# A graph layer on one core: the last group of edges gets an order of its own

## The chip, the cores and the metric

The kernel runs on one NeuronCore of a Trainium2 chip. The core has five engines with instruction queues of their own: TensorE (PE in the profile, its weight loads as PEld), VectorE (DVE), ScalarE (ACT), GpSimd (POOL) and SyncE (SP). SP, ACT and POOL also issue DMAs, which 16 DMA engines carry out. The metric is the device time of one execution in microseconds (us), lower is better; of several runs the median is taken.

## What is computed

A message-passing layer on a graph with 6250 nodes of 128 features and 206250 edges, sorted by receiver, and a residual with a layer norm behind it:

```
w_ij  = silu(edge_feats @ rad_W1 + rad_b1) @ rad_W2 + rad_b2
w_ij += silu(chi_scalar @ sph_W1 + sph_b1) @ sph_W2 + sph_b2
q_i = (x @ Wq)[receivers];  k_j = (x @ Wk)[senders];  v_j = (x @ Wv)[senders]
alpha = (q_i * w_ij * k_j).sum(over the 16 of a head) / sqrt(16) * cutoffs
out = segment_sum(alpha * v_j, receivers) / 16
result = layernorm(x + out)
```

There are 8 heads of 16. `edge_feats` and `chi_scalar` are the two arrays of 206250 x 32 edge attributes, `cutoffs` the edge weights. Everything is float32.

## The kernel before

**Tiles.** 128 edges are a tile, 4 tiles a quad (512 edges), 4 quads a group (2048 edges). The 206250 edges make 403 quads and 101 groups (`NG`); the last group, 100, has three quads: 400, 401 and 402. A group's quads are worked in the order 0, 2, 1, 3 (`order`), so the last three are 400, 402, 401. As the edges are sorted by receiver, the receivers of a quad lie within a window of 32 nodes (`W`), and those of a group within one of 128, and the windows of neighbouring groups overlap.

**First stage.** A table `kv_tab` with the keys and values of all nodes is made and stored in HBM; those of the first ten quads are made from gathered rows of x instead.

**Main loop** (from line 603, over groups and the four slots of each). All instructions are issued in an order written out by hand; each engine runs its own in that order and waits by semaphore for the others. In the iteration of quad `order[i]`:
- TensorE works the first layers of quad i+2 (`first_layers`, L408), fetches the queries of quad i+1 to its edges with a one-hot product (`q_at_edges`, L419) and works the second layers of quad i+1 (`weigh`, L450 and L455).
- ACT takes the SiLU of quad i+2 (`silus`, L440).
- DVE multiplies query and key of quad i+1 (`multiply`, L462, reads the gathered `kv`), and then of quad i multiplies by the weights, sums over the heads, scales (`scores`, L469 to L473) and makes the messages (`messages`, L484).
- POOL gathers the 4 x 128 rows of `kv_tab` for quad i+14 (`gathers`, L120, `AHEAD`), each row gather after a signal of TensorE from quad i.
- In slots 1 to 3 TensorE sums the messages of the group before into the windows of its quads (`sum_quads`, L495, one-hots of 32 columns from `one_hots`); ACT copies the sums (`part_sums`, L524).

**From sums to rows.** `place(g)` makes two matrices on DVE (L518, L519) that move a group's four windows, and the total of the group before it, into the group's window of 128 rows. `sum_group(g)` multiplies with them on TensorE (L529, L531), and ACT copies the total `tot` (L533). `statistics(g)` adds x and takes mean and variance on DVE (L541 to L544). Four groups are a batch (`LB`): after the fourth, ACT takes the square roots (L547), DVE reciprocal and shift (L549, L551), and ACT scales the rows (L554). The batches are groups 0 to 3, 4 to 7 and so on up to 92 to 95; then 96 and 97 together, then 98, 99 and 100 each alone. The square root and SiLU need different function tables on ACT, so each batch brings a table load before its square root and another before the next SiLU. `write_rows` lets SP write a group's 128 rows to `out` (L561), one group a slot. Since the windows overlap, each write waits for the one before it to land.

**The last group** is handled by conditions on `last` in the same loop. Its quads aren't summed into windows of 32: `wide_one_hots(q)` (L503, L504, L507) makes one-hots of 128 columns, kept in buffers of the tag `act`, and `sum_wide` (L511) sums straight into the 128 rows of the group. The wide one-hots are made at the end of slot 3 of group 99 (quad 400), in slot 0 (402) and in slot 1 (401) of the last group; `place(99)` in slot 0, `place(100)` (one matrix) in slot 1. There also stands the load of a verdict into a register of each engine (line 658): whether the inputs are of the assumed form; if not, a slower general path follows. In the last group's slot 2 quad 402 is finished, with the statistics of group 98. Behind the loop (line 672 on) come the sums of group 99, the last quad's scores and messages in two halves (its multiply was done whole before), the statistics of group 99 between the halves, and the statistics and the write of group 100 (L708, L710).

Of the kernel before, what the change touches and what calls it, by code (L numbers as in the profile page):

```python
# [24 lines left out]
P = 128  # L25
# [29 lines left out]
def gnn_kernel(ctx, tc, x, src, dst, weight, edges, rad_W1, rad_b1, rad_W2, rad_b2,  # L55
# [310 lines left out]
    with tc.tile_pool(name="ps", bufs=1, space=PSUM) as pp:  # L366
# [93 lines left out]
        def multiply(q, mark=None):  # L460
            kq_of[q] = quad_of("kq", 3)
            o = nc.vector.tensor_tensor(kq_of[q], pq_of[q], kv_of[q][:, :, :D], op=OP.mult)  # L462
            if mark is not None:
                after(o, mark)
# [34 lines left out]
        def wide_one_hots(q):  # L499
# [5 lines left out]
            hot_of[q, "wide"] = ep.tile([P, EQ], F32, name="act", bufs=8).rearrange(  # L505
# [8 lines left out]
        def place(g):  # L514

            to = to_of[g] = gp.tile([P, 2, P], F32, name="to")
# [18 lines left out]
        def statistics(g):  # L535
            first = g // LB * LB if g < NG - 3 else g
            if g == first:
                y0_of[g] = (gp.tile([P, LB, D], F32, name="y0"), gp.tile([P, LB, 2], F32, name="mv"))
            y0, mv = y0_of[first]
            k = g - first + 1  # L540
            nc.vector.tensor_tensor(y0[:, k - 1, :], tot_of[g], x_of[g], op=OP.add)  # L541
            st = gp.tile([P, 6], F32, name="st")
            nc.vector.bn_stats(st, y0[:, k - 1, :])
            nc.vector.bn_aggr(mv[:, k - 1, :], st)  # L544
            if k == LB or g >= NG - 4:
                sd = gp.tile([P, LB], F32, name="sd")
                nc.scalar.activation(sd[:, :k], mv[:, :k, 1], AF.Sqrt, bias=eps)  # L547
                rs = gp.tile([P, LB], F32, name="rs")
                nc.vector.reciprocal(rs[:, :k], sd[:, :k])  # L549
                shift = gp.tile([P, LB], F32, name="shift")  # L550
                nc.vector.scalar_tensor_tensor(shift[:, :k], mv[:, :k, 0], -1.0, rs[:, :k],  # L551
                                               op0=OP.mult, op1=OP.mult)
                for i in range(k):
                    nc.scalar.activation(y0[:, i, :], y0[:, i, :], AF.Identity,  # L554
                                         scale=rs[:, i:i + 1], bias=shift[:, i:i + 1])
                    written.append((first + i, y0[:, i, :]))
# [46 lines left out]
        for g in range(NG):  # L603
            last = g == NG - 1
            for slot, j in enumerate((0, 2, 1, 3)):
                q = g * NQ + j
                i = g * NQ + slot
                if q >= QUADS:
                    continue
# [3 lines left out]
                if slot == 0 and g + 1 < NG:  # L613
# [3 lines left out]
                if slot == 2 and g + 1 < NG:  # L617
                    turned = make_q(g + 1)
                if 1 <= g:
                    for t in ((), (0, 1), (2, 3))[slot] if last else ((), (0, 1), (2,), (3,))[slot]:  # L620
                        mark = sum_quads(g - 1, t)
                if last and slot == 2:
                    po_of[g] = pp.tile([P, EQ], F32, name="ph", bufs=2)[:, :D]
                    for t in range(QT):
                        sum_wide(order[i - 2], t, start=(t == 0))
                if i + 2 < len(order):
                    first_layers(order[i + 2])
                if i + 1 < len(order):
                    mark = q_at_edges(order[i + 1])
                    marks = weigh(order[i + 1])  # L630
                if i + 2 < len(order):
                    silus(order[i + 2], mark, marks)
# [6 lines left out]
                if i + 1 < len(order):  # L639
                    multiply(order[i + 1], mark)  # L640
                    messages(q, scores(q, marks=marks), marks=marks)
# [6 lines left out]
                if slot == 1:  # L648
                    if g + 1 < NG:
                        one_hots_T(g + 1)  # L650
                    if g + 2 < NG:
                        pick(g + 2)
                    if 1 <= g < NG - 1:
# [215 lines left out]
```

## Time and profile before

| | us |
|---|---|
| median of 3 runs | 2042.45 (2042.1 to 2043.92) |
| the run that was profiled | 2043.99 |
| its span, from the first to the last instruction | 2042.2 |
| busy: PE | 1843.1 (90%) |
| busy: PEld | 1527.2 (75%) |
| busy: DVE | 1466.9 (72%) |
| busy: ACT | 720.1 (35%) |
| busy: POOL | 1529.6 (75%) |
| DMA engines, mean share | 50% (queue of gathers 36.1%, of SP's transfers 13.8%) |

A page of the profile has the busy time of each engine, the groups of instructions, the chain of work that ended last, and the waits. A line of the groups reads: source line, engine, operation, the tile written and those read, shapes, count, then busy us and the mean ns of one, and after the last bar the idle time of the engine just before them with what ended most of it. A line of the timeline reads: start in us from the span's beginning, duration, engine, source line, operation, tiles, shapes, count, and in square brackets the idle time before it and what ended it. A line of the waits reads: who waited for what, us in total, how many times, the longest. On the span's last stretches the table by windows gives these busy times and granted TensorE clocks:

| us from the start | PE | DVE | ACT | POOL | granted clock |
|---|---|---|---|---|---|
| 1980 to 2000 | 18.06 | 13.62 | 9.93 | 15.12 | 0.83 |
| 2000 to 2020 | 17.37 | 14.23 | 6.19 | 15.12 | 1.00 |
| 2020 to 2042.2 | 11.06 | 14.94 | 6.92 | 2.53 | 0.80 |

### The profile page before, as it was taken

Reading aid. Unit: us, or ns where it says so; the run is one execution under the profiler, and the core shown is the slowest. Engines: PE = TensorE matmul, PEld = TensorE weight load, DVE = VectorE, ACT = ScalarE, POOL = GpSimd, SP = SyncE. Lnnn points to the kernel's source line nnn. Section 1 sums busy time; section 2 is a strip of 40 time slices with the busy share of each in tenths; the row PEclk is TensorE's granted clock in tenths of the full one; section 3 lists DMA queues with packets and bytes.
Section 4 is the critical chain, followed back from the end, with each engine's and each line's share of the span. In section 5 each row is a group of like instructions: output and inputs, shape, how many; then the busy total and the mean of one; then the engine's idle time right before and its main releaser. Section 6 shows DMA issues by size and latency. Waiting matters only on the chain.

```text
span 2042.2 us, 44162 instructions
## 1 busy us (share of the span) xinstructions
PE 1843.1 (90%) x16011; PEld 1527.2 (75%) x16011; DVE 1466.9 (72%) x3005; ACT 720.1 (35%) x1425; POOL 1529.6 (75%) x1620
## 2 busy tenths in 40 slices
PE   9999998889899999898999989898998999898987
PEld 7788887777777777777777777777776777777776
DVE  6698887677767677677767667776766767677766
ACT  2334443333333323333333333233333333333333
POOL 7777777777777777777777777777777777777774
PEclk9899999899898898899888988998989989989889
DMA  8555554545445544545454554445454544544452
GB/s 309 149 150 154 154 157 145 153 136 152 140 147 141 153 146 142 146 143 152 136 151 142 149 148 145 146 142 148 140 152 136 153 140 148 151 143 147 140 149 81
DMA packets 141371, 304.03 MB, mean 149 GB/s; under 512 B 34028, under 2 KB 73820, under 8 KB 141148
## 3 DMA queue, kind: packets, MB, share of 16 engines
q0 software_dynamic: 76736, 208.77, 36.1%
q1 hardware_dynamic: 62912, 92.00, 13.8%
q8 instruction: 127, 2.08, 0.4%
q14 instruction: 96, 0.79, 0.1%
q10 hardware_dynamic: 1500, 0.40, 0.1%
HBM read 287.58 MB, written 13.46 MB: 147 GB/s over the span
## 4 chain that ended last, share of the span: by engine, by line
PE 50%; DMA 19%; DVE 14%; issue 7%; ACT 4%; POOL 4%; DVEq 0%; POOLq 0%; ACTq 0%
PE pw L455 24%; DMA kv<-kv_tab,src_i 19%; PE pq L419 10%; PE ph L408 7%; DVE kq L462 5%; PE po L495 4%; DVE side L471 2%; DVE kq L469 2%; PE pw L450 2%; POOL kv L120 2%; POOL msg L120 2%; ACT y L554 2%; ACT L440 2%; PE pq L388 1%; PE pq L529 1%
## 5 line engine op out<-in xcount | busy, mean ns | idle before, releaser
L120 POOL DMA_INDIRECT kv<-kv_tab,src_i x1572 | 1489.9, 948 | 479.7 <-issue 188.9
L440 ACT ACTIVATE act<-ph,b 128x512 f32<-128x512 f32 x806 | 518.7, 685 | 1176.6 <-PE pq L419 1149.0
L455 PE MATMUL pw<-w,act 128*128 128x128 f32 x6448 | 911.1, 300 | 0.1
L455 PEld LDWEIGHTS pw<-w,act 128*128 128x128 f32 x6448 | 830.1, 208 | 105.5 <-issue 93.2
L462 DVE TENSOR_TENSOR kq<-pq,kv 128x512 f32<-128x512 f32 x403 | 277.6, 689 | 401.6 <-DMA kv<-kv_tab,src_i 225.1
L419 PE MATMUL pq<-q,hotT 32*128 32x128 f32 x3224 | 498.1, 297 | 29.6 <-DVE kq L462 28.8
L408 PE MATMUL ph<-feats,w 32*128 32x512 f32 x1612 | 502.6, 681 | 23.3 <-ACT act L440 23.3
L419 PEld LDWEIGHTS pq<-q,hotT 32*128 32x128 f32 x3224 | 419.2, 199 | 87.0 <-issue 57.7
L471 DVE TENSOR_REDUCE side<-kq 128x32 f32<-128x512 f32 x404 | 279.9, 693 | 41.6
L484 DVE TENSOR_TENSOR msg<-kv,side 128x512 f32<-128x512 f32 x404 | 277.3, 686 | 43.4 <-DVE side L473 1.2
L469 DVE TENSOR_TENSOR kq<-pw,kq 128x512 f32<-128x512 f32 x404 | 274.1, 678 | 0.0
L408 PEld LDWEIGHTS ph<-feats,w 32*128 32x128 f32 x1612 | 137.6, 193 | 106.4 <-issue 59.6
L450 PE MATMUL pw<-brow,onesb 3*128 3x512 bf16 x403 | 161.1, 400 | 1.1 <-DVE kq L469 1.1
L495 PE MATMUL po<-msg,hot 128*32 128x128 f32 x3200 | 155.8, 292 | 0.0
L529 PE MATMUL pq<-part,to 128*128 128x128 f32 x200 | 45.6, 311 | 94.4 <-DVE kq L462 62.1
L473 DVE TENSOR_TENSOR side<-side,scale 128x32 f32<-128x32 f32 x404 | 80.6, 199 | 42.2 <-DVE side L471 0.5
L529 PEld LDWEIGHTS pq<-part,to 128*128 128x128 f32 x200 | 30.5, 192 | 106.8 <-issue 63.2
L495 PEld LDWEIGHTS po<-msg,hot 128*32 128x32 f32 x3200 | 71.4, 111 | 38.7 <-issue 5.3
L388 PE MATMUL pq<-wq,xT 128*128 128x128 f32 (+1 forms) x202 | 47.5, 320 | 37.3 <-DVE kq L462 36.9
L394 DVE TENSOR_TENSOR hotT<-relb,side 128x512 f32<-128x512 bf16 x101 | 68.7, 680 | 0.0
L388 PEld LDWEIGHTS pq<-wq,xT 128*128 128x128 f32 (+1 forms) x202 | 34.6, 214 | 45.6 <-DVE kq L462 44.9
L399 DVE TENSOR_TENSOR hot<-rel,side 128x512 f32<-128x512 f32 x100 | 66.1, 661 | 0.0
(107 smaller groups left out, 832.0 us busy)
## 6 DMA issues: line engine op xcount, KB each, us to landing
feats<-in_edges SPq DMA_DIRECT2D x101, 512.0 KB
kv<-kv_tab,src_i POOLq DMA_INDIRECT x1572
relb<-rel_lin SPq DMA_DIRECT2D x101, 128.0 KB
x<-in_x SPq DMA_DIRECT2D x101, 64.0 KB
out<-y SPq DMA_DIRECT2D x101, 64.0 KB
kv_tab<-kv SPq DMA_DIRECT2D x12, 512.0 KB
act<-in_x SPq DMA_DIRECT2D x12, 256.0 KB
dst_i<-in_dst SPq DMA_DIRECT2D x1, 808.0 KB
```

Of the source, the lines that this page charges most:

```text
L120: return nc.gpsimd.indirect_dma_start(out=o, out_offset=None, in_=table, in_offset=bass.IndirectOffsetOnAxis(ap=index, axis=0))
L388: nc.tensor.matmul(pt[:n, :D], xT_of[g][:, :n], wq, start=True, stop=True)
L408: return nc.tensor.matmul(act_of[q, i], w1[r0:r0 + R, :], feats_of[g][r0:r0 + R, c0:c0 + EQ], start=True, stop=True)
L419: o = nc.tensor.matmul(pq_of[q][:, t, :], hotT_of[g][b, t * P:(t + 1) * P], q_of[g][b, :], start=True, stop=True)
L440: o = nc.scalar.activation(act, act_of[q, i], AF.Silu, bias=b1[:, i:i + 1])
L450: nc.tensor.matmul(pw, onesb, brow.rearrange("p t d -> p (t d)"), start=True, stop=False)
L455: o = nc.tensor.matmul(pw[:, t, :], act_of[q, i][:, t * P:(t + 1) * P], w2[:, i, :], start=False, stop=(t == QT - 1 and i == 1))
L462: o = nc.vector.tensor_tensor(kq_of[q], pq_of[q], kv_of[q][:, :, :D], op=OP.mult)
L469: nc.vector.tensor_tensor(m, pw_of[q][:, t, :], m, op=OP.mult)
L471: o = nc.vector.tensor_reduce(alpha, m.rearrange("p t (h e) -> p t h e", e=HD), AX.X, OP.add)
L484: o = nc.vector.tensor_tensor(msg_of[q][:, t, :].rearrange("p t (h e) -> p t h e", e=HD), kv_of[q][:, t, D:].rearrange("p t (h e) -> p t h ...
L495: o = nc.tensor.matmul(po_of[g][j * W:(j + 1) * W, :], hot_of[g][:, j * QT + t, :], msg_of[g * NQ + j][:, t, :], start=(t == 0), stop=(t = ...
```

## The change

- The main loop runs over groups 0 to 99 only, without the conditions on `last`. The work of the last group follows the loop, in an order of its own.
- The wide one-hots have a tag of their own (`wide`, three buffers). They are made in slot 0 (quad 400) and slot 2 (402) of group 98 and in slot 0 of group 99 (401). The register load stands behind the last of them.
- `place(100)` is made in slot 2 and `place(99)` in slot 3 of group 99. The matrix of group 100 has a buffer of its own (`to_end`).
- `statistics` is cut into `moments` (sum, mean and variance), `roots` (ACT's square roots) and `normalize` (reciprocal, shift, scaling). The batches are counted from the end: group 0 alone, 1 to 4, 5 to 8, up to 93 to 96; 97 to 100 share a buffer, but each is normalized alone in the last part.
- In the last part the quads 400, 402 and 401 are a, b and c. In the first stretch DVE multiplies b, does the messages of a and normalizes 97; before, 96 and 97 had been normalized in the loop. Then come the messages of b (ahead of the multiply of c, before they came behind it), the moments of 98, and c in halves, its multiply too: first half, normalizing 98, moments of 99, second half, normalizing 99, moments and scaling of 100. Group 98 had been normalized ahead of c's halves, and 99 ahead of c's last messages.
- On TensorE the sums of group 98 and the first half of group 99's come behind the second layers of b, where they came ahead of those of c; the second half of group 99's sums and the wide sums of a behind the second layers of c.

The diff, with the two parts of the loop's conditions that went cut out:

```diff
-        def multiply(q, mark=None):
-            kq_of[q] = quad_of("kq", 3)
-            o = nc.vector.tensor_tensor(kq_of[q], pq_of[q], kv_of[q][:, :, :D], op=OP.mult)
+        def multiply(q, mark=None, t=slice(0, QT)):
+            if t.start == 0:
+                kq_of[q] = quad_of("kq", 3)
+            o = nc.vector.tensor_tensor(kq_of[q][:, t, :], pq_of[q][:, t, :], kv_of[q][:, t, :D],
+                                        op=OP.mult)
...
-            hot_of[q, "wide"] = ep.tile([P, EQ], F32, name="act", bufs=8).rearrange(
+            hot_of[q, "wide"] = ep.tile([P, EQ], F32, name="wide", bufs=3).rearrange(
...
-            to = to_of[g] = gp.tile([P, 2, P], F32, name="to")
+            to = to_of[g] = gp.tile([P, 2, P], F32, name="to" if g < NG - 1 else "to_end",
+                                    bufs=2 if g < NG - 1 else 1)
...
-        def statistics(g):
-            first = g // LB * LB if g < NG - 3 else g
+        def first_of(g):
+            return max(g - (g - (NG - LB)) % LB, 0)
+        def moments(g, total):
+            first = first_of(g)
...
+            nc.vector.tensor_tensor(y0[:, k, :], total, x_of[g], op=OP.add)
             st = gp.tile([P, 6], F32, name="st")
+            nc.vector.bn_stats(st, y0[:, k, :])
+            nc.vector.bn_aggr(mv[:, k, :], st)
+        def roots(a, b):
...
+            nc.scalar.activation(sd[:, :b - a], y0_of[first][1][:, a - first:b - first, 1], AF.Sqrt,
+                                 bias=eps)
+        def normalize(a, b, sd):
...
+            nc.vector.reciprocal(rs[:, :n], sd[:, :n])
...
+            nc.vector.scalar_tensor_tensor(shift[:, :n], mv[:, a - first:b - first, 0], -1.0, rs[:, :n],
+                                           op0=OP.mult, op1=OP.mult)
+            for g in range(a, b):
...
+                nc.scalar.activation(y, y, AF.Identity, scale=rs[:, g - a:g - a + 1],
+                                     bias=shift[:, g - a:g - a + 1])
+                written.append((g, y))
+        def statistics(g):
+            moments(g, tot_of[g])
+            if g < NG - LB and first_of(g + 1) > g:
+                normalize(first_of(g), g + 1, roots(first_of(g), g + 1))
...
-        for g in range(NG):
-            last = g == NG - 1
+        for g in range(NG - 1):
...
+                if g == NG - 3 and slot in (0, 2):
+                    wide_one_hots(order[slot // 2 - 3])
+                if g == NG - 2 and slot == 0:
+                    wide_one_hots(order[-1])
+                    n = nc.values_load(general, min_val=0, max_val=1)
+                if g == NG - 2 and slot == 2:
+                    place(NG - 1)
+                if g == NG - 2 and slot == 3:
+                    place(g)
+        g, (a, b, c) = NG - 1, order[-3:]
+        first_layers(c)
+        mark = q_at_edges(b)
+        marks = weigh(b)
+        turned = sum_group(g - 2)
+        for t in range(QT // 2):
+            sum_quads(g - 1, t)
+        silus(c, mark, marks)
+        sd = roots(g - 3, g - 2)
+        turned()
+        multiply(b, mark)
+        messages(a, scores(a, marks=marks), marks=marks)
+        normalize(g - 3, g - 2, sd)
+        write_rows()
+        mark = q_at_edges(c)
+        marks = weigh(c)
+        for t in range(QT // 2, QT):
+            sum_quads(g - 1, t)
+        po_of[g] = pp.tile([P, EQ], F32, name="ph", bufs=2)[:, :D]
+        for t in range(QT):
+            sum_wide(a, t, start=(t == 0))
         part_sums(g - 1)
-        sum_group(g - 1)()
+        turned = sum_group(g - 1)
+        messages(b, scores(b, marks=marks), marks=marks)
+        moments(g - 2, tot_of[g - 2])
+        sd = roots(g - 2, g - 1)
+        turned()
         for t in range(QT):
-            sum_wide(order[-2], t)
+            sum_wide(b, t)
         nc.tensor.matmul(po_of[g], to_of[g][:, 1, :], tot_of[g - 1], start=False, stop=False)
...
+        multiply(c, mark, halves[0])
+        messages(c, scores(c, halves[0]), halves[0])
+        for t in range(QT // 2):
+            sum_wide(c, t)
+        normalize(g - 2, g - 1, sd)
+        write_rows()
+        moments(g - 1, tot_of[g - 1])
+        sd = roots(g - 1, g)
+        multiply(c, mark, halves[1])
+        messages(c, scores(c, halves[1]), halves[1])
+        for t in range(QT // 2, QT):
+            sum_wide(c, t, stop=(t == QT - 1))
+        normalize(g - 1, g, sd)
+        write_rows()
+        moments(g, po_of[g])
+        sd = roots(g, g + 1)
...
+        ys, mv = y0_of[first_of(g)]
+        y = ys[:, LB - 1, :]
-        nc.vector.tensor_scalar(y, y, mv[:, 1, 0:1], rs[:, 1:2], op0=OP.subtract, op1=OP.mult)
+        nc.vector.tensor_scalar(y, y, mv[:, LB - 1, 0:1], rs[:, 0:1], op0=OP.subtract, op1=OP.mult)
         nc.sync.dma_start(out[N - P:, :], y)
```

More of the change, by code (lines that the diff above doesn't have):

```diff
@@ L539, in statistics @@
             y0, mv = y0_of[first]
-            k = g - first + 1
-            nc.vector.tensor_tensor(y0[:, k - 1, :], tot_of[g], x_of[g], op=OP.add)
+            k = g - first
+            nc.vector.tensor_tensor(y0[:, k, :], total, x_of[g], op=OP.add)
             st = gp.tile([P, 6], F32, name="st")
[L543 to L556, printed above, removed]
+            nc.vector.bn_stats(st, y0[:, k, :])
```

82 lines of the change are left out of this document (23 added, 59 removed).

## The prediction

> **What bounds it now.** I read the groups of the page first, then the waits and the timeline of POOL, then the timeline of DVE at the end, then the waits of SP. a, b and c are the three quads of the last group, in the order in which they are worked (400, 402, 401).
>
> The gathers are the costliest thing outside TensorE, and POOL issues nothing else:
>
> ```profile
> L120 POOL DMA_INDIRECT kv<-kv_tab,src_i x1572 | 1489.9, 948 | 479.7 <-issue 188.9
> ```
>
> and its timeline ends with
>
> ```profile
> 2018.45 0.94 POOL L120 DMA_INDIRECT kv<-kv_tab,src_i  x1 [0.30 <-issue]
> ...
> 2022.20 0.95 POOL L120 DMA_INDIRECT kv<-kv_tab,src_i  x1 [0.31 <-issue]
> ```
>
> 479.7 us of idle time over 1572 gathers is 0.305 each, and 0.30 stands before every single one in the timeline: POOL never waits for anybody, it issues a gather each 1.25 us from 2.9 us on (40 of x, then 1572) to 2022.20. Four a quad are 5.01 us. TensorE is busy 90%, but where the gathers are still far ahead 41 multiplies, from 125.3 to 289.8, follow one another at 4.0 us: it could do a quad in less than POOL's 5.01, and its share does not make it the bound. DVE shows it: the multiply (L462) waits for its quad's last gather.
>
> ```profile
> 2010.05 0.69 DVE L462 TENSOR_TENSOR kq<-pq,kv 128x512 f32<-128x512 f32 x1 [0.36 <-DMA kv<-kv_tab,src_i]
> ...
> 2015.05 0.69 DVE L462 TENSOR_TENSOR kq<-pq,kv 128x512 f32<-128x512 f32 x1 [1.82 <-DMA kv<-kv_tab,src_i]
> ...
> 2020.08 0.69 DVE L507 TENSOR_TENSOR act<-d,side 128x512 f32<-128x512 f32 x1
> 2020.68 0.68 DVE L462 TENSOR_TENSOR kq<-pq,kv 128x512 f32<-128x512 f32 x1
> ...
> 2024.24 0.69 DVE L507 TENSOR_TENSOR act<-d,side 128x512 f32<-128x512 f32 x1
> 2024.84 0.35 DVE L518 TENSOR_SCALAR to<-side,rowq 128x128 f32<-128x128 f32 x1
> ...
> 2028.91 0.69 DVE L507 TENSOR_TENSOR act<-d,side 128x512 f32<-128x512 f32 x1
> ...
> 2030.96 0.16 DVE L549 RECIPROCAL rs<-sd 128x1 f32<-128x1 f32 x1 [0.36 <-ACT sd L547]
> ...
> 2033.18 0.29 DVE L683 TENSOR_TENSOR y<-tot,x 128x128 f32<-128x128 f32 x1 [0.39 <-ACT tot L533]
> ...
> 2035.18 0.42 DVE L484 TENSOR_TENSOR msg<-kv,side 128x256 f32<-128x256 f32 x1
> 2036.81 0.29 DVE L683 TENSOR_TENSOR y<-ph,x 128x128 f32<-128x128 f32 x1 [1.22 <-PE ph L511]
> ...
> 2038.21 0.35 DVE L708 TENSOR_SCALAR y<-y,mv,rs 128x128 f32<-128x128 f32 x1
> ```
>
> Up to 2020 the gathers set the pace. From b's multiply (2020.68) to the last message (2035.18) DVE runs without a pause longer than 0.4 us: that stretch, not the gathers, sets the end. Behind it come TensorE's last sums (1.22), the last statistics and the last write, which has a wait of its own:
>
> ```profile
> SPq L710 <- DMA out<-y: 2.9, 1, 2.9
> ```
>
> and in its timeline
>
> ```profile
> 2039.20 0.34 SPq L710 DMA_DIRECT2D out<-y  x1
> ```
>
> L708 ends at 2038.56, yet the write leaves at 2039.20: writes of rows follow one another, and group 99's, issued at 2035.87, had landed only then. So 0.64 us there belong to a DMA. From 2039.20 to the span's end at 2042.2 are 3.0.
>
> **What lies under cover.** Anything that leaves POOL's row of gathers alone and is done by some 2020 us costs nothing. The loop's changes are of that kind: three wide one-hots (rows L503, L504, L507: 0.20 + 0.26 + 0.61 = 1.07 us each) and three placing matrices (0.26 each) move to groups 98 and 99, where DVE waits 0.4 to 2.2 us a quad for gathers. Without that cover they would cost what they cost now. The register load of the verdict (0.46 to 0.54 us on each of five queues) moves five quads forward; on POOL it stays behind the last gather, since gathers are queued 14 quads ahead, and on SP it stands ahead of writes that aren't due. No DMA is added, and the count of row writes stays at 101. Group 0 becomes a batch of one, groups 1 to 96 batches of four: the square-root table is loaded 26 times before (24 batches, 96 with 97, 98) and 26 times after (0, 24 batches, 97). An early batch can't hold gathers up: they run up to 14 quads behind TensorE's signals, and after 75.26 us POOL shows no wait above 0.31.
>
> **The batch moves closer to the end.** Before, the last batch of four (92 to 95) sits at 1978; after, 93 to 96 sit one group, 20.05 us, later. What a batch does to the multiplies:
>
> ```profile
> 1986.24 0.69 DVE L462 TENSOR_TENSOR kq<-pq,kv 128x512 f32<-128x512 f32 x1 [2.90 <-PE pq L419]
> ...
> 1992.86 0.69 DVE L462 TENSOR_TENSOR kq<-pq,kv 128x512 f32<-128x512 f32 x1 [2.16 <-DMA kv<-kv_tab,src_i]
> ...
> 1995.96 0.68 DVE L462 TENSOR_TENSOR kq<-pq,kv 128x512 f32<-128x512 f32 x1
> ...
> 2000.37 0.68 DVE L462 TENSOR_TENSOR kq<-pq,kv 128x512 f32<-128x512 f32 x1
> ...
> 2005.39 0.69 DVE L462 TENSOR_TENSOR kq<-pq,kv 128x512 f32<-128x512 f32 x1 [1.84 <-DMA kv<-kv_tab,src_i]
> ```
>
> Against the gathers (issue of a quad's last one + 2.87) these are late by 1.3, 2.9, 1.0, 0.4 and 0.4 us. Moved by 20.05 they are quads 398 to 400, b and c: b comes as the fourth, 0.4 late or less, because the load of features that runs in the second row's stretch isn't there in the last group. DVE: multiply of 400 at 2015.5 at the latest (1995.96 + 20.05 = 2016.0 less 0.5 of that load), 3.09 to the end of messages, 0.75 for the statistics of 97, 0.52 for placing 99: free at 2019.9. b's last gather is issued at 2017.20. In the chain of waits the two quads before it land 2.75 after issue, this one 3.29. So b's multiply starts at 2020.1 (2.75 + 0.12) to 2020.6; I take 2020.1, with the two. Before: 2020.68.
>
> **The stretch after it**, in start-to-start times of the rows of the last 22 us: multiply 0.605; scores and messages of a quad 0.785 + 0.80 + 0.305 + 0.60 = 2.49; moments 0.32 + 0.33 + 0.10 = 0.75; reciprocal and shift 0.28; a half of scores and messages 0.45 + 0.465 + 0.22 + 0.34 = 1.475. A half of the multiply has no row: not under the 0.34 of the half-width L484, not over the 0.605 of the whole; I take 0.34 (same width; up to 0.5 more in all). After:
> - multiply b and messages a 3.095, normalize 97 0.28, messages b 2.49, moments 98 0.75: 6.615
> - first half of c 1.815, normalize 98 0.28, moments 99 0.75: 2.845
> - second half up to the start of its messages 1.475
>
> Together 10.935. Before it was 2035.18 - 2020.68 = 14.50. What goes: two wide one-hots 2.14, three placing matrices 0.78, two waits of 0.36 and 0.39 and a few gaps; what comes: normalize 97 and a second start of the multiply. Gain 3.565, and 0.58 from the earlier start: 4.15.
>
> The waits that it adds: normalize 97 on DVE needs ACT's square root, with messages b queued behind it. ACT has silus of c by 2020.2, the table 1.28, the root 0.30: 2021.8, against 2023.2 on DVE. Moments 99 needs tot of 99 (TensorE's L529 after part sums: 1.42 us from part to moments now), with over 2 us in hand. c's own gathers land at 2022.20 + 2.75 = 2024.95, its first half starts at 2026.7.
>
> **The end.** Last message to L708's end 2.96 + 0.42, as now. Normalize 99 now comes behind the last message, so group 99's write leaves later against it: 0.77 + 0.49 + 0.03 after the message's start instead of 0.69. If that write takes 1.55 (98's now, issued at 2031.87, by the trace's record of completions: its 16 parts landed 1.35 to 1.53 after issue) the last one isn't held up at all and 0.6 more is won; if one part straggles as now (3.27; the other 15 had landed after 1.52), it is held as long as now or 0.6 longer. I keep 0.64. Sum: 2042.2 - 4.15 = 2038.05 of span. The profiled run took 2043.99, 1.79 more than its span, and the median of the runs is 2042.45; taken from the median: **2038.3**, 0.20% faster. All low ends together give 2037.7 (no straggler), all high ones 2039.9 (b at 2020.6, dear halves, the longer hold).
>
> [...] The casts and scalar operations of the wide one-hots now all run beside gathers. Before, L503 and L504 at 2019.62 and 2019.82 ran beside the gathers of 2018.45 and 2019.70, which kept their 1.25 us, as did those beside L518 at 2009.09. [...]
>
> **Rivals.**
> 1. *b starts late* (0.22). Over the 19 earlier batches the quad in b's place was 0.3 late or more in 12, at worst 2.5, and here one-hots are added. b at 2020.6 to 2022.5 gives 2038.8 to 2040.7: inside 0.2%. Against it: no feature load.
> 2. *Writes in a row* (0.07). 98's is due 9.38 after b's multiply, 99's 12.2, 100's 14.35; at 3.27 each the last leaves at 16.0, end 19.0 after b: gain 3.1, 2039.3. For it: L710's wait; against: 1.53 for 98's.
> [...]
> 4. *TensorE stays slow after the batch* (0.08), the other side. After each batch one quad's L455 takes 3.3 to 3.8 us instead of 2.05 (1905.95: 3.78) at a granted clock of 0.83. If that lasted, quads would take 4.4 + 1.7 = 6.1 against 5.01, and the lateness of 399 would grow instead of shrinking: 2.9 + 2 x 1.1 = 5.1 at b, 2025.2, end 2043.4; from the worst batch seen (4.4) 6.6, end 2044.9; with c's weights 1.7 late as well, 2046.6. From 4.2 late at b on the change loses. Against: 2.05 again in the next quad, each time.
>
> Forecast 0.60. 0.2% (4.1 us) is about what a measurement of this kernel can tell from no change, and the forecast lies just beyond; faster 0.60, same 0.22 + 0.07 + 0.03 and the milder half of the fourth, 0.04, = 0.36, slower 0.04. Range 2037.1 to 2040.8, which leaves out the worst of 1 and 4.
>
> **What would show it.** Last gather at 2022.2 again; b's multiply at 2020.1 to 2020.6; no gap on DVE from there to c's last message at 2031.0; L507 three times before 2005; L710 at 2035.05, or 2034.5 if nothing straggles. A gather spacing above 1.25 at L507, or b's multiply released by PE, proves me wrong.

## The result and the profile after

| | before | after |
|---|---|---|
| median of 21 runs each, us | 2042.57 (2041.26 to 2044.59) | 2039.56 (2037.95 to 2041.97) |
| ratio, with its 95% interval | | 0.9985 (0.9978 to 0.9991) |
| span of the profiled execution, us | 2042.2 | 2039.3 |
| issue of the last gather | 2022.20 | 2022.38 |
| from there to the span's end (called the tail below) | 20.02 | 16.92 |

The change makes the kernel 3.0 us faster, 0.15%. The forecast was 2038.3; the time is 1.26 above it and inside the range. At 0.15% it lies on the near side of the 0.2% that was called a distinguishable difference, so of the three cases it is the one called the same, though with 21 runs each the interval leaves 1 out.

First the groups of the page. The row of the gathers has the count and nearly the duration of before, but its idle time has other releasers:

```profile
L120 POOL DMA_INDIRECT kv<-kv_tab,src_i x1572 | 1488.0, 947 | 482.0 <-PE pw L455 188.9
```

482.0 over 1572 is still 0.307 each. A sum cannot show one long wait among 1572 short ones, and there is one. In the timeline of POOL between 70 and 80 us, of after:

```profile
73.22 0.95 POOL L120 DMA_INDIRECT kv<-kv_tab,src_i  x1 [0.30 <-issue]
77.49 0.94 POOL L120 DMA_INDIRECT kv<-kv_tab,src_i  x1 [3.33 <-PE pw L455]
78.74 0.95 POOL L120 DMA_INDIRECT kv<-kv_tab,src_i  x1 [0.31 <-PE pw L455]
...
2022.38 0.94 POOL L120 DMA_INDIRECT kv<-kv_tab,src_i  x1 [0.30 <-PE pq L534]
```

and of before at the same gather:

```profile
75.26 0.95 POOL L120 DMA_INDIRECT kv<-kv_tab,src_i  x1 [0.89 <-PE pw L455]
```

This is the first gather that waits for a signal of TensorE from the main loop; the 3.33 are TensorE's late start, and nothing that the change touches runs there. Most of the lateness arises in the 24 products at 55.3 us, of after

```profile
55.26 7.04 PE L229 MATMUL pk<-wkv,xT 128*128 128x256 f32 x24
```

and of before

```profile
55.38 5.35 PE L229 MATMUL pk<-wkv,xT 128*128 128x256 f32 x24
```

where TensorE's granted clock, from 55 to 62.5 us, was 0.77 in the one and 1.00 in the other. The two executions reach the last gather 0.18 apart all the same, because from 100 us on the gathers of after followed one another at 1250.7 ns on average and those of before at 1252.0, over some 1535 gathers 2.0 us. That the two nearly cancel is luck.

The end, in DVE's timeline of after (the multiply is L463 now, messages L486, the wide one-hot's comparison L509, the last scaling L734):

```profile
2004.60 0.69 DVE L509 TENSOR_TENSOR wide<-d,side 128x512 f32<-128x512 f32 x1
2006.74 0.69 DVE L463 TENSOR_TENSOR kq<-pq,kv 128x512 f32<-128x512 f32 x1 [1.46 <-PE pq L419]
...
2012.83 0.69 DVE L463 TENSOR_TENSOR kq<-pq,kv 128x512 f32<-128x512 f32 x1 [1.78 <-PE pq L419]
...
2016.44 0.69 DVE L463 TENSOR_TENSOR kq<-pq,kv 128x512 f32<-128x512 f32 x1 [0.16 <-PE pq L419]
...
2020.90 0.69 DVE L463 TENSOR_TENSOR kq<-pq,kv 128x512 f32<-128x512 f32 x1
...
2027.51 0.40 DVE L463 TENSOR_TENSOR kq<-pq,kv 128x256 f32<-128x256 f32 x1
...
2030.52 0.40 DVE L463 TENSOR_TENSOR kq<-pq,kv 128x256 f32<-128x256 f32 x1
2032.10 0.42 DVE L486 TENSOR_TENSOR msg<-kv,side 128x256 f32<-128x256 f32 x1
2033.83 0.29 DVE L548 TENSOR_TENSOR y<-ph,x 128x128 f32<-128x128 f32 x1 [1.05 <-PE ph L513]
2035.09 0.17 DVE L731 RECIPROCAL rs<-sd 128x1 f32<-128x1 f32 x1 [0.42 <-ACT sd L556]
2035.29 0.35 DVE L734 TENSOR_SCALAR y<-y,mv,rs 128x128 f32<-128x128 f32 x1
```

The last wide one-hot is made at 2004.60, and from b's multiply (2020.90) to c's last message (2032.10) no line has a bracket: DVE runs through. That stretch was 14.50 and is 11.20. What stands ahead of it is the batch of groups 93 to 96: the multiplies at 2006.74, 2012.83 and 2016.44 wait for TensorE, no longer for their gathers. The last write, in the waits and the timeline of SP's queue:

```profile
SPq L735 <- DMA out<-y: 2.0, 1, 2.0
```

```profile
2035.73 0.34 SPq L735 DMA_DIRECT2D out<-y  x1
```

It leaves 0.09 after the end of L734, where the one of before was held 0.64, but then 3.57 pass to the span's end, where 3.0 had passed.

### The profile page after: what moved, and what is told of

Read it like the earlier page. It is cut to its first block, busy times and chain, and to the rows that moved or that the text cites. A ratio compares the mean times of both kernels' runs of the same rounds, so it can differ in the third digit from the quotient of the medians.

```text
span 2039.3 us, 44163 instructions
## 1 busy us (share of the span) xinstructions
PE 1839.6 (90%) x16011; PEld 1525.5 (75%) x16011; DVE 1469.2 (72%) x3008; ACT 719.9 (35%) x1426; POOL 1527.4 (75%) x1620
## 4 chain that ended last, share of the span: by engine, by line
PE 51%; DMA 20%; DVE 13%; issue 8%; ACT 4%; POOL 4%; DVEq 0%; POOLq 0%; ACTq 0%
PE pw L455 25%; DMA kv<-kv_tab,src_i 19%; PE pq L419 9%; PE ph L408 7%; DVE kq L463 5%; PE po L497 4%; DVE side L473 2%; POOL kv L120 2%; PE pw L450 2%; DVE kq L471 2%; POOL msg L120 2%; ACT L440 2%; ACT y L570 1%; PE pq L388 1%; PE pq L532 1%
## 5 line engine op out<-in xcount | busy, mean ns | idle before, releaser
L120 POOL DMA_INDIRECT kv<-kv_tab,src_i x1572 | 1488.0, 947 | 482.0 <-PE pw L455 188.9
L455 PE MATMUL pw<-w,act 128*128 128x128 f32 x6448 | 906.1, 299 | 0.0
L455 PEld LDWEIGHTS pw<-w,act 128*128 128x128 f32 x6448 | 825.8, 208 | 102.2 <-issue 89.5
L463 DVE TENSOR_TENSOR kq<-pq,kv 128x512 f32<-128x512 f32 x404 | 278.1, 688 | 394.3 <-DMA kv<-kv_tab,src_i 240.0
L486 DVE TENSOR_TENSOR msg<-kv,side 128x512 f32<-128x512 f32 x404 | 277.5, 687 | 43.8 <-DVE side L475 1.4
```

Source lines behind the costliest of these rows:

```text
L120: return nc.gpsimd.indirect_dma_start(out=o, out_offset=None, in_=table, in_offset=bass.IndirectOffsetOnAxis(ap=index, axis=0))
L455: o = nc.tensor.matmul(pw[:, t, :], act_of[q, i][:, t * P:(t + 1) * P], w2[:, i, :], start=False, stop=(t == QT - 1 and i == 1))
L463: o = nc.vector.tensor_tensor(kq_of[q][:, t, :], pq_of[q][:, t, :], kv_of[q][:, t, :D], op=OP.mult)
L486: o = nc.vector.tensor_tensor(msg_of[q][:, t, :].rearrange("p t (h e) -> p t h e", e=HD), kv_of[q][:, t, D:].rearrange("p t (h e) -> p t h ...
```

## The experiments

The question was which parts made the 3 us, and why 1.1 of the forecast gain was missing. Twelve kernels ran in three lots, each beside the kernel before on the same chip (the second and the third lot had one chip). Medians, in us:

| label | kernel | median | before beside it | ratio (95%) |
|---|---|---|---|---|
| e1_batches_front | after, batches as before | 2615.56 | 2617.44 | 0.9984 (0.9966 to 1.0001) |
| e2_early_hots | before, early one-hots and matrices | 2614.03 | 2617.44 | 0.9979 (0.9960 to 0.9998) |
| e3_c_ahead | after, c's multiply whole and ahead of b's messages | 2617.98 | 2617.44 | 0.9995 (0.9977 to 1.0012) |
| e4_late_hots | after, one-hots and matrices where they were | 2621.11 | 2617.44 | 1.0007 (0.9987 to 1.0026) |
| e5_spread_pad | after, other rows for the padded edges | 2039.94 | 2042.87 | 0.9986 (0.9977 to 0.9996) |
| e6_free_start | after, first gathers free of signals | 2037.58 | 2042.87 | 0.9973 (0.9962 to 0.9983) |
| e7_c_whole | after, c not in halves | 2039.22 | 2042.87 | 0.9981 (0.9971 to 0.9990) |
| e8_three | e1 + e5 + e6 | 2037.68 | 2042.87 | 0.9975 (0.9964 to 0.9986) |
| e9_before_free | before, first gathers free of signals | 2042.03 | 2043.50 | 0.9989 (0.9980 to 0.9999) |
| e10_early_free | e2 + e6 | 2039.88 | 2043.50 | 0.9983 (0.9973 to 0.9993) |
| e11_front_free | e1 + e6 | 2038.28 | 2043.50 | 0.9973 (0.9963 to 0.9983) |
| e12_free_again | e6 once more | 2038.63 | 2043.50 | 0.9976 (0.9966 to 0.9986) |

**The first lot** ran on a chip whose TensorE got a lower clock. By cores, span and mean granted clock of e1:

```profile
core 0: 2616.6 us, clock 0.811
```

At 0.811 instead of 0.922 TensorE, not POOL, sets the pace: in e1 POOL sits idle 524.9 us until TensorE's second layers (L455), in waits of up to 23.2 (in before 174.1, none over 0.9), the last gather is issued some 70 us before the end, and all rows lie ready long before they are multiplied. So what these four were expected to do to the tail could not be seen there. DVE's own order in the last stretch can be: nothing in it waits for a gather on that chip.

e1 counts the batches from the front again; 96 to 100 then share a buffer and 96 and 97 are normalized together in the last part:

```diff
-            return max(g - (g - (NG - LB)) % LB, 0)
+            return min(g // LB * LB, NG - 1 - LB)
...
-        sd = roots(g - 3, g - 2)
+        sd = roots(g - 4, g - 2)
...
-        normalize(g - 3, g - 2, sd)
-        write_rows()
+        normalize(g - 4, g - 2, sd)
+        write_rows(2)
```

> The changed kernel with the batches counted from the front as before (92 to 95 the last one in the loop; 96 and 97 normalized together behind the first messages of the last part). Measured on the tail, from the issue of the last gather to the span's end: 20.0 us before, 16.9 after. Theory 1 (the batch moved one group towards the end makes b's multiply late): b's multiply starts 2.9 us after the issue of its quad's last gather instead of 3.5, tail 16.3. Theory 2 (b's last gather itself lands late, 3.29 us after issue before and 3.40 after, against 2.75 for its neighbours, whatever the batches): b's multiply still 3.4 to 3.5 after, tail 16.8 to 16.9. In both, no change against the changed kernel that a time of some 2039.5 us can tell.

Measured: the stretch from b's multiply to the last message is 11.19, as in after; b's multiply came 57.6 us behind its own last gather, so this lot says nothing on whether the batch or the gather holds it. The question went to the second and third lots.

e2 is the kernel before with the one-hots and matrices of the changed kernel and nothing else of it. The lines that come in, without the new buffers and without the old places that go:

```diff
+                if g == NG - 3 and slot in (0, 2):
+                    wide_one_hots(order[slot // 2 - 3])
+                if g == NG - 2 and slot == 0:
+                    wide_one_hots(order[-1])
+                    n = nc.values_load(general, min_val=0, max_val=1)
+                if g == NG - 2 and slot == 2:
+                    place(NG - 1)
+                if g == NG - 2 and slot == 3:
+                    place(g)
```

> The kernel before with one part of the change alone: wide one-hots and placing matrices made early, in buffers of their own. Theory 1 (DVE's stretch sets the end, but c's multiply stands ahead of b's messages and can't start before c's last gather has landed, 2.75 us after its issue): c's multiply 2.9 us after the last gather's issue instead of 3.16, and only the one-hot of c and the last matrix (1.33) behind it are won; tail 20.0 - 0.3 - 1.3 = 18.4. Rival (all that leaves the stretch is won, 2.14 + 0.78): tail 17.1. Rival (DVE is not what sets the end): 20.0.

Measured: stretch 11.59, against 14.50 in the profile of the kernel before (at clock 0.92): 2.91 less, which is the 2.14 + 0.78 = 2.92 of the rows. With every row at hand, the moved instructions give back what they cost.

e3 undoes the order of b's messages and c's multiply, and the halving of that multiply:

```diff
+        multiply(c, mark)
         messages(b, scores(b, marks=marks), marks=marks)
...
-        multiply(c, mark, halves[0])
...
-        multiply(c, mark, halves[1])
```

> The changed kernel with c's multiply whole and ahead of b's messages, as it stood before. Theory (the new order fills the wait for c's gather with b's messages): DVE waits some 0.9 us for c's gather, the halves' second start of the multiply (0.3) is saved; tail 17.4 to 17.6. Rival (the order of these two is indifferent): 16.6.

Measured: stretch 10.91, 0.29 shorter than with the halves. Where c's rows are early the old order costs nothing, and the halved multiply is the dearer one. e10 below shows the same order where the rows are late.

e4 is the mirror of e2: the whole change, but the one-hots of 402 and 401 and the matrices in the last stretch again, and the one-hot of 400 right ahead of it. Of its diff, the lines in the last stretch:

```diff
         messages(a, scores(a, marks=marks), marks=marks)
+        wide_one_hots(b)
+        place(g - 1)
...
         messages(b, scores(b, marks=marks), marks=marks)
+        wide_one_hots(c)
+        place(g)
```

> The changed kernel with the wide one-hots and the placing matrices made where they were (one-hot of a behind the statistics of 97, of b with the matrices of 99 behind a's messages, of c with that of 100 behind b's messages). Theory (DVE's stretch sets the end): two one-hots and three matrices, 2.92, come back into it and b's multiply starts up to 0.5 later; tail 19.8 to 20.4. Rival (the gain comes from the order of the last part): 17 to 17.5.

Measured: stretch 14.09 = 11.19 + 2.90. In its DVE timeline two of the three comparisons stand between b's multiply (2587.57) and c's first half:

```profile
2587.57 0.68 DVE L463 TENSOR_TENSOR kq<-pq,kv 128x512 f32<-128x512 f32 x1
2591.13 0.69 DVE L509 TENSOR_TENSOR wide<-d,side 128x512 f32<-128x512 f32 x1
2595.47 0.69 DVE L509 TENSOR_TENSOR wide<-d,side 128x512 f32<-128x512 f32 x1
2597.08 0.40 DVE L463 TENSOR_TENSOR kq<-pq,kv 128x256 f32<-128x256 f32 x1
```

So what the early one-hots take off DVE's stretch is settled twice over.

**The second lot**, and the third, got a granted clock of 0.92 to 0.93, as the profiles of before and after did.

e5. The 206250 edges leave 86 places of the last quad (402, which is b) unfilled; they are padded, with weight zero. The kernel pads the senders with the last one, so that with the last edge's own 87 of the 128 rows of b's last gather are one and the same; e5 pads them with senders from the front of the list. As the weight is zero, the output does not depend on it. (The expectation's 118 should be 86.)

```diff
-        "src": _columns(inputs["src"], "edge"),
+        "src": _columns(inputs["src"], "wrap"),
```

> The changed kernel with other sources for the 118 padded edges behind the last real one (their weight is zero, so they add nothing): the first edges' sources instead of the last source 118 times. b's last tile is 86 of 128 rows padding, so its gather reads one row 87 times. In all six traces so far that gather landed 2.9 to 3.5 us after its issue, on both kinds of chip. Theory (the repeated row slows it): it lands like its neighbours, 2.5 to 2.8. Where the gathers set the pace (clock 0.92) b's multiply then starts at most 0.1 earlier, as DVE is ready only then (2020.86 in the changed kernel); at clock 0.81 nothing changes. Rival (an instruction fetch or the writes of rows slow it): 3.2 to 3.5 again.

Measured: b's last gather lands 2.76 after its issue, against 3.40 in after. Its DVE timeline (the gather was issued at 2015.35):

```profile
2013.47 0.69 DVE L463 TENSOR_TENSOR kq<-pq,kv 128x512 f32<-128x512 f32 x1 [0.16 <-PE pq L419]
...
2018.24 0.69 DVE L463 TENSOR_TENSOR kq<-pq,kv 128x512 f32<-128x512 f32 x1 [0.36 <-DMA kv<-kv_tab,src_i]
```

The multiply comes 2.89 after the issue, nearly the 2.87 of the quads that wait for their gathers, and DVE still waits 0.36 for it: the batch had not made b late. In after the rows landed at 2020.78, and 0.12 later the multiply began; DVE had been ready at 2020.86, so that the two bounds met: in that execution the batch had made DVE late too. The time of e5, 2.93 below its before, cannot be told from the 3.01 of the change: 0.65 is under what ten runs with a spread of 1 us resolve.

e6 lets the gathers of the first three iterations go without TensorE's signal:

```diff
-                    gathers(order[i + AHEAD], old[-QT:])
+                    gathers(order[i + AHEAD], old[-QT:] if i > 2 else ())
```

> The changed kernel with the first three quads' gathers of the loop (quads 14 to 16) freed of the wait for TensorE's signal. Theory (POOL waits for TensorE once, at 73 to 77 us: 0.6 us in the profiled run of before, 3.0 in that of the changed kernel, and what it loses there stays lost, as gathers set the pace to the end): no pause on POOL above 0.31 there, the last gather 0.6 to 3.0 us earlier, the median 1 to 3 us lower than the changed kernel's on a chip with clock 0.92. Rival (the wait is made up later): the same time. On a chip with clock 0.81, where gathers run ahead all the time: no change in both.

Measured: 2037.58, 5.29 below its before instead of 3.01. POOL's timeline has no pause left at the place where after had 3.33:

```profile
74.36 0.95 POOL L120 DMA_INDIRECT kv<-kv_tab,src_i  x1 [0.30 <-issue]
75.62 0.95 POOL L120 DMA_INDIRECT kv<-kv_tab,src_i  x1 [0.30 <-issue]
76.87 0.95 POOL L120 DMA_INDIRECT kv<-kv_tab,src_i  x1 [0.30 <-issue]
```

The tail is 17.0, as in after; the last gather goes at 2018.88 instead of 2022.38. And the runs lie between 2036.79 and 2038.22, where after's lie between 2037.95 and 2041.97; in the lot of e6, e5 and e7, which have the wait, spread by 1.03 and 1.09 us (standard deviation, SD), e6 by 0.45: the wait at the start was most of the spread from run to run.

e7 leaves the last quad whole throughout, its multiply, scores and messages:

```diff
-        multiply(c, mark, halves[0])
-        messages(c, scores(c, halves[0]), halves[0])
...
+        multiply(c, mark)
...
-        multiply(c, mark, halves[1])
-        messages(c, scores(c, halves[1]), halves[1])
...
+        messages(c, scores(c))
```

> The changed kernel with the last quad whole instead of in halves (multiply, scores, messages and sums; moments of 99 ahead of its scores). From the start of b's multiply to the start of the last message it takes 10.1 to 10.4 us instead of 11.2. Theory (the halves hide TensorE's first two sums behind DVE): the last message is 0.27 longer and the sums behind it 0.5 to 1.0, so from b's multiply to DVE's end 14.6 to 15.1 against 14.74: no gain from halves worth a time. Rival (halves pay): 15.3 or more. Rival (whole is better): 14.2 or less.

Measured: 2039.22, 3.65 below its before. In DVE's timeline:

```profile
2018.93 0.69 DVE L463 TENSOR_TENSOR kq<-pq,kv 128x512 f32<-128x512 f32 x1 [0.66 <-DMA kv<-kv_tab,src_i]
...
2028.90 0.69 DVE L486 TENSOR_TENSOR msg<-kv,side 128x512 f32<-128x512 f32 x1
2031.75 0.29 DVE L548 TENSOR_TENSOR y<-ph,x 128x128 f32<-128x128 f32 x1 [1.90 <-PE ph L513]
```

The last message starts 9.97 after b's multiply instead of 11.20 (10.1 to 10.4 had been expected), but takes 0.69 and is followed by four tiles' sums instead of two (1.90 of waiting instead of 1.05). From b's multiply to the end of the last scaling it is 14.63, in after 14.74, both with the last sums at a granted clock of 0.5. The halves win nothing, here or by the times.

e8 puts the front batches, the other padding and the free start together.

> The changed kernel with three edits together: batches counted from the front, other sources for the padding, and the first three quads' gathers free of TensorE's signal. On a chip with clock 0.92: b's multiply 2.9 us after its last gather's issue, tail from the last gather's issue 16.2 to 16.4 instead of 16.9, last gather 0.6 to 3.0 earlier: 2036 to 2038.5. With clock 0.81: the changed kernel's time.

Measured: 2037.68, not to be told from e6. The tail is 16.79, not the 16.2 to 16.4 expected. The batches did what they were to do, and b's multiply nevertheless came late:

```profile
2011.38 0.69 DVE L463 TENSOR_TENSOR kq<-pq,kv 128x512 f32<-128x512 f32 x1 [1.08 <-DMA kv<-kv_tab,src_i]
...
2016.93 0.69 DVE L463 TENSOR_TENSOR kq<-pq,kv 128x512 f32<-128x512 f32 x1 [1.13 <-DMA kv<-kv_tab,src_i]
```

3.42 after its gather's issue (2013.51), in spite of the padding. By the trace's records of DMA packets and completions 15 of that gather's 16 parts had landed after 2.78, and one after 3.30; a fetch of instructions, 16 KB in 0.95 us from 2014.50 on, had ended at 2015.45, just where that part's late packets begin.

**The third lot** repeats the question with the start's noise taken out. All four have the edit of e6; beside it e9 is the kernel before, e10 has the edit of e2, e11 that of e1, and e12 is e6 again. (The expectations call TensorE's signals marks.)

> The kernel before, with the first three iterations' gathers free of TensorE's marks, and nothing else. Theory (POOL's wait at the start belongs to both kernels, and varies from execution to execution): no wait of POOL over 0.4 us, last gather at 2018.5 to 2019.0, tail from the last gather's issue to the span's end 20.0 as before, times 2040.4 to 2041.2 with a spread (SD) of 0.5 against 1.06. Rival (the change brought its own wait at the start, before had next to none): 2041.9 to 2042.6, at most 0.9 us saved.

> The kernel before with its three wide one-hots and the placing matrices made two groups sooner, its old order of the last group, whole multiplies and old batches kept, and the start free of marks as above. Theory (what the change won is the 2.92 us of one-hots and matrices that left the last stretch of DVE; the new order and the halves are worth nothing): tail 17.0 to 17.4, times 2037.3 to 2038.1, within 0.4 of the whole change with a free start. Rival (the order of b and c and the halved multiply win 0.7 by themselves, as the sum of the prediction had it: 4.15 less 2.92 less the stall): 2038.3 to 2038.8.

> The changed kernel with its batches counted from the front as before, and the start free of marks. Theory A (the batch of groups 93 to 96 makes b's multiply late, by 0.2 to 0.8): b's multiply released by its own gather, 2.87 to 3.42 after that gather's issue, tail 16.2 to 16.8, times 2036.9 to 2037.5. Theory B (b's gather lands late anyway, so the batch costs nothing): 2037.3 to 2037.9, within 0.3 of the whole change with a free start.

> The whole change with the start free of marks, once more, as the yardstick of the three others on their chip. Both theories: 2037.2 to 2038.0, spread (SD) 0.4 to 0.6, last gather at 2018.5 to 2019.0, tail 16.8 to 17.2 where TensorE's granted clock is 0.92.

Measured, the ten runs of each (nine of e11) with a spread (SD) of 0.5, so that a difference of two medians is known to about 0.56 (two times 0.5 times the root of 2/10, and a quarter more for medians than for means):

- before to e9: 1.47 won (0.6 either way). No wait of POOL above 0.31 is left in e9, so the wait at the start belongs to the kernel before too. But e9's time came 0.8 above its range and inside the rival's, in a lot where the kernel before was slower as well (2043.50), and the rival's gain of at most 0.9 is not clearly out. Its last gather (2020.02) and its tail (20.76) are longer than expected.
- e9 to e12: 3.40. This is the change itself, without the start.
- e9 to e10: 2.15 of it are the early one-hots and matrices.
- e10 to e12: 1.25 are all the rest, order, halves and batches. e10's time (2039.88) is above the ranges of both theories, and its tail is 18.20 instead of 17.0 to 17.4; but e12's is above its own too. Measured against e12, the theory that they are worth nothing (within 0.4) is out, and the rival's 0.7 is at the edge of the uncertainty.
- e12 to e11: 0.35 less with the batches of before, within the uncertainty. Both are above their ranges. Theory B, that the batch costs nothing, fits; by the times alone a few tenths for the batch can't be ruled out. In both profiles b is released by its own late gather, 3.45 after its issue in e11 and 3.34 in e12:

```profile
2018.36 0.69 DVE L463 TENSOR_TENSOR kq<-pq,kv 128x512 f32<-128x512 f32 x1 [1.16 <-DMA kv<-kv_tab,src_i]
```

e12 is the kernel of e6 on the same chip, and its median is 1.05 higher, 0.6 above its range; its last gather goes at 2019.79 instead of 2018.5 to 2019.0, and its tail is 16.22 instead of 16.8 to 17.2. So times are compared here within a lot alone, and tails of single profiles to no better than half a us.

Why early one-hots do not give their full 2.92 in e10 is seen in its DVE timeline (L462 is the multiply in this kernel):

```profile
2018.61 0.69 DVE L462 TENSOR_TENSOR kq<-pq,kv 128x512 f32<-128x512 f32 x1 [0.64 <-DMA kv<-kv_tab,src_i]
...
2021.10 0.69 DVE L484 TENSOR_TENSOR msg<-kv,side 128x512 f32<-128x512 f32 x1
2022.79 0.69 DVE L462 TENSOR_TENSOR kq<-pq,kv 128x512 f32<-128x512 f32 x1 [1.00 <-DMA kv<-kv_tab,src_i]
```

Freed of the one-hots, DVE reaches c's multiply before c's rows are there (last gather issued at 2019.95, multiply 2.84 later) and stands for 1.00. Its stretch is 12.69, against 15.02 in e9, 2.33 less. On the first chip, where the rows were early, the same line in e2 had no gap. The new order puts the 2.49 of b's messages into that hole: e12's DVE has no wait between b's multiply and the last message, its stretch is 11.20 against e10's 12.69.

```profile
2018.13 0.69 DVE L463 TENSOR_TENSOR kq<-pq,kv 128x512 f32<-128x512 f32 x1 [0.61 <-DMA kv<-kv_tab,src_i]
...
2029.33 0.42 DVE L486 TENSOR_TENSOR msg<-kv,side 128x256 f32<-128x256 f32 x1
2030.55 0.29 DVE L548 TENSOR_TENSOR y<-ph,x 128x128 f32<-128x128 f32 x1 [0.54 <-PE ph L513]
```

e10 has three waits there that e12 has not: this 1.00, 0.36 for the root of group 98 and 0.39 for tot of group 99. Against them e12 has the 0.28 of normalizing 97 and the dearer halves of c's multiply.

## Why the prediction came out as it did

**What held.** POOL's row, a gather each 1.25 us, sets the pace up to b. The last gather at 2022.2 (2022.38) holds by luck, since a start that was 2.2 later was made up by a quicker pace. No gap on DVE from b to the last message. All three one-hots before 2005 (1983.83, 1995.09, 2004.60), on cover. The 0.03 in the sum of the chances stands for gathers held up by two one-hots, 1.07 us each; no run shows that: in after the gathers beside all three kept their 1.25 us. Rival 4, TensorE staying slow, was not seen (the 3.78 us of L455 at 1905.95 ran at a granted clock of 0.50, not 0.83): against the gathers (issue of a quad's last one + 2.87) the multiplies from 2006.74 on were late by 1.5, 2.6, 1.2 and 0.65 us, so that the lateness rose once and then fell. The moved 2.92 was measured as 2.91 and 2.90.

**What failed, by terms of the sum** (forecast gain of span 4.15, profiled pair 2.90):

| term | forecast | measured | difference |
|---|---|---|---|
| b's multiply starts, against 2020.68 | 2020.1 | 2020.90 | 0.80 |
| b's multiply to the last message | 10.935 | 11.20 | 0.26 |
| last message to the last scaling's end | 3.38 | 3.54 | 0.16 |
| last scaling's end to the last write | 0.64 | 0.09 | -0.55 |
| last write to the span's end | 3.0 | 3.57 | 0.57 |

The first is the step that failed: "b's last gather is issued at 2017.20 ... So b's multiply starts at 2020.1 (2.75 + 0.12) to 2020.6; I take 2020.1, with the two". The issue came at 2017.38 and the landing 3.40 after it, so the choice between 2.75 and 3.29 went to the wrong row. The 3.29 was b's own gather in the profile of before, the 2.75 were others', and b's is not like others: it holds the padded edges. With the padding it lands 3.20 to 3.54 after its issue in all eight profiles at clock 0.92, without it 2.76 in e5 (and in e8 but for one part behind a fetch): the padding makes it late. The batch was named as the danger, in the text and in rival 1, whose time (2038.8 to 2040.7) holds the result. In the profile of after it came true beside the late gather: DVE was ready at 2020.86, 3.48 after the issue, instead of the forecast 2019.9, so that there a gather on time would have won next to nothing. In e5, e6, e7 and e12, with the batch in the same place, DVE was ready 2.5 to 2.75 after the issue, as forecast (2.70), and b waited 0.36 (e5) to 0.69 for its gather; and e11 wins nothing certain by moving the batch away. Which of the two holds b in the median execution is not shown.

The second is a mis-sized term: a half multiply was put at 0.34 with up to 0.5 more allowed in all. Start to start it took 0.51 and 0.44; e3's stretch, with the multiply whole, is the check, 0.29 shorter.

The third depends on the clock of the execution: it took 3.54 where half was granted for TensorE's last sums, as in after, and 3.03 where all was, as in e5 and e12 (the last section).

The last two nearly cancel, by luck. The write of group 99 was issued at 2033.34 and landed at 2035.66, so the last one was hardly held: the forecast kept the hold and named its absence as the low end. But the last write itself took 2.01 to land instead of the 1.57 of before, with a packet of queue q14 ("instruction" on the page) among its parts. The 0.09 belongs to this execution. In e5, e6, e8, e11 and e12 the last write is held 0.41 to 1.02, leaving 0.06 to 0.07 after group 99's has landed: there the end is set by that write, whose last part is late in every profile, and not by TensorE's last sums. Rival 2, writes in a row, is right in that much.

**What the forecast did not see** is the wait at the start. That 0.30 stands before every gather and that "POOL never waits for anybody" is wrong by one line; "after 75.26 us POOL shows no wait above 0.31" is true of the profile of before. The line at 75.26 itself, 0.89 for TensorE, was read as the end of the beginning and not as a price that changes from execution to execution. Against the kernel before beside them, e6 and e12 put it at 2.28 and 1.86 us for the changed kernel (5.29 and 4.87 less 3.01), and e9 at 1.47 for the one before. It is in both, so that it hardly moves the difference, but it makes the spread.

Without it the change is worth 3.40 (0.56 either way), the forecast 4.15. The difference is of the size of the 0.65 of b's gather and the 0.26 of the halves; that these two are all of it is not shown, as e5 did not resolve its 0.65 in the time.

The best kernels tried are those of the change with the first gathers free of signals, e6 (and e12), e8 and e11: 4.87 to 5.29 below the kernel before beside them, not to be told apart.

## What to carry to other kernels

Work taken off the engine that sets the end is worth its duration only up to the next wait: here 2.92 us of one-hots and matrices gave 2.15, until the order was changed so that other work stood where the rows were late. Where a queue's row of equal steps runs through the whole kernel, as POOL's 1.25 us do here, a pause at its beginning can come out at the end (without the 3.33 of after, e6 issued its last gather 3.50 sooner), so look for its first wait, not for its mean. And take the price of a transfer from the row of that very transfer, where it has one: b's gather took 3.29 in before and 3.40 in after, not the 2.75 of the others.

## What the hardware showed

- The page counts fetches of instructions among the packets of the 16 DMA engines, as queues of their own. Of after:

```profile
q8 instruction: 127, 2.08, 0.4%
```

  That is packets, MB and share of the 16 engines' span. One fetch of this queue is 16 KB and takes 0.9 to 1.9 us, half of them up to 1.0. Of two transfers in 16 parts one part landed late behind a fetch: in e8 that of b's last gather (3.30 after issue, the others up to 2.78), and in before, group 99's write had 15 of 16 parts landed 1.52 after its issue and the last at 3.27: a fetch at 2036.75 took 1.32, and that part's packets run from 2038.05 to 2038.52. In all 14 profiles a fetch falls on that write, and its last part lands 2.32 to 3.40 after issue.
- A gather in which 87 of 128 rows are the same one landed later: 3.20 to 3.54 us after issue instead of the 2.76 of e5, with its 16 parts landing one after another from 2.4 on instead of together.
- The granted clock has two levels in the records of all 14 traces, 1.0 and 0.5 (in before 61 records of each, in after 55), and the stretches of the half fell elsewhere in each execution. On the last four multiplies it was 0.50 in after,

```profile
2032.57 1.23 PE L513 MATMUL ph<-msg,wide 128*128 128x128 f32 x4 [2.23 <-DVE msg L486]
```

  and 1.00 in e12, the same last part of the kernel:

```profile
2029.80 0.71 PE L513 MATMUL ph<-msg,wide 128*128 128x128 f32 x4 [2.23 <-DVE msg L486]
```

  DVE then waits 1.05 in the one and 0.54 in the other; the profiles of the changed kernel in halves have the one or the other (1.05 in e1, e4, e6 and e8, 0.54 in e3, e5 and e11), as the clock there is half or full.
- Two chips gave one and the same kernel 2043 and 2617 us, at mean granted TensorE clocks of 0.92 and 0.81: on the second TensorE is the bound (the 524.9 us that POOL waits for it in e1), and the tail that this change works on is hidden there. The means are mixtures of the two levels: in before 322 of 2039 us are at half, in e1 989 of 2614. Why the second chip has the half more often, no run shows.
